# A two-layer graph network on one core: all weight loads on SyncE, and a later, wider placing of the second layer's attention chain

## The chip, the cores and the metric

The kernel runs on one NeuronCore of one Trainium2 chip. The metric is the device time of one execution in microseconds. Engines are named as in the profile: PE (TensorE), DVE (VectorE), ACT (ScalarE), POOL (GpSimd), SP (SyncE, which here only issues DMAs).

## The reference

There are 64 independent graphs of 256 nodes with 256 features, and a 256 x 256 adjacency matrix each. Two layers run one after the other on every graph, in float32.

```python
# layer 0: relational multi-head attention (8 heads of 32, 4 relations), then a feed-forward block
q, k = x @ Wq + bq, x @ Wk + bk                    # split into heads
attn = softmax(q @ k.T / sqrt(32))                 # per head
out = sum over r of (attn * (adj == r)) @ (x @ Wv[r] + bv[r])
x = LN(x + out @ Wo + bo)
x = LN(x + gelu(x @ W1 + b1) @ W2 + b2)            # 256 -> 1024 -> 256
# layer 1: two graph attentions with single scores, then a feed-forward block
def gat(h, W, a):
    Wh = h @ W
    e = leaky_relu(Wh @ a[:256] + (Wh @ a[256:]).T, 0.2)
    return softmax(where(adj > 0, e, -9e15), axis=1) @ Wh   # softmax over the row index
h = LN(x + gat(gat(x, W1', a1), W2', a2))
out = LN(h + relu(h @ w_ff1 + b1) @ w_ff2 + b2)
```

## The kernel before

Every graph is one object with a list of steps (load, x_by_feature, queries_keys, values, scores, maximum, exponential and so on). Each step issues a few instructions, mostly a PE product and the operation that takes its result out of PSUM. The method `timetable` gives every step a due time, graph g's times being shifted by g times 60. All steps of all graphs are sorted by due time (ties by order of entry) and issued in that order; every engine then runs its own instructions strictly in that order and waits by semaphores. So the due times are no clock. They only fix the order in which the steps of neighbouring graphs are interleaved: in the middle of the run, four graphs at different stages share each period.

Steps that matter here, with their lines in the kernel before:

- Weights: the helpers `weight`, `rowvec` and `colvec` (L87 to L101) and the loads in L117 to L142 each issue a DMA into a constant tile. Before, ACT issues them all, SP issues the loads of x and adj (`load_front`, L103), the residual `y` (L389) and the stores (L465).
- Layer 0: `xT` and `hT`, `ffa_T`, `ffb_T` are transposes on PE (L188) copied by ACT (L189). `qk_ps` (L302), `v_ps` (L313, evacuated by DVE in L316), scores `s` (L326), maxima `nmax` (L332, DVE), exponentials `e` (L340, ACT), reciprocals `rden` (L345, DVE), normalisation (L350, POOL), transposes of e (L356, PE), the copy `es` (L362, ACT), the masked products `pm` (L364, DVE) and the last one (L369, POOL), `po` (L380, PE; `heads_out`), `wo_ps` (L398, PE; its result is added into y by DVE, L400).
- Feed-forward blocks: ffa belongs to layer 0 (Gelu), ffb to layer 1 (Relu). `up` is L240 on PE with its activation L243 on ACT, two of eight blocks a step; `down` is L249, eight steps; `end` is L253.
- Norms (`Norm`): `stats` (L203 to L207, DVE), `root` (L211, POOL), `apply` (L216 and L220, two each, DVE). x1 and x2 follow layer 0's two halves, x3 and o layer 1's.
- Layer 1's attention chain: `gat_first` makes hT from ffa_res; `gat_product` makes `ga_wps` (L411) and its copy `ga_wh` (L413); `gat_scores` is `ga_ips` on PE (L420) and z on ACT (L423); `gat_mask` is three DVE operations (L427, L428, L430); `gat_exponential` is Exp on ACT (L435); `gat_divide` is a reciprocal and two scalings on DVE (L441, L443). `gat_second` is the product h1 on PE (L451) and its copies on ACT (L453); scores, mask, exponential and divide come again for the second attention (names gb), and `gat_out` is the product h2 (L460), added by DVE (L462).

All PE results of these steps but the scores and the accumulators of `down` share three PSUM buffers (`mm_tile`, L71), which are given out in turn.

Of the kernel before, what the change touches and what calls it, by code (L numbers as in the profile page):

```python
# [17 lines left out]
P = 128  # L18
# [5 lines left out]
def _row(ap, n):  # L24

    return bass.AP(tensor=ap.tensor, offset=ap.offset, ap=[[0, P], [1, n]])


def _col(ap, n):

    return bass.AP(tensor=ap.tensor, offset=ap.offset, ap=[[1, P], [P, n // P]])
# [3 lines left out]
def kernel(  # L35
# [12 lines left out]
    nc = tc.nc  # L48
    B, N, D = x.shape
# [4 lines left out]
    KD = D // P  # L54
# [32 lines left out]
    def weight(w, name):  # L87
        k, n = w.shape[0] // P, w.shape[1]
        t = const.tile([P, k, n], F32, name=name)
        nc.scalar.dma_start(t, w.rearrange("(k p) n -> p k n", p=P))  # L90
        return t

    def rowvec(v, n, name):
        t = const.tile([P, n], F32, name=name)
        nc.scalar.dma_start(t, _row(v, n))
        return t

    def colvec(v, n, name):
        t = const.tile([P, n // P], F32, name=name)
        nc.scalar.dma_start(t, _col(v, n))  # L100
        return t  # L101

    def load_front(g):  # L103
# [5 lines left out]

    loaded = {0: load_front(0)}  # L110
    wq, wk = weight(Wq, "wq"), weight(Wk, "wk")
    bq_c, bk_c = colvec(bq, D, "bq_c"), colvec(bk, D, "bk_c")
    scale = 1.0 / math.sqrt(DH)
    bqs_c = const.tile([P, KD], F32, name="bqs_c")
    nc.vector.tensor_scalar(bqs_c, bq_c, scale, None, op0=ALU.mult)

    wv = const.tile([P, KD, KD, R, P], F32, name="wv")  # L117
    for k in range(KD):
        for m in range(KD):
            nc.scalar.dma_start(  # L120
                wv[:, k, m], Wv[:, k * P:(k + 1) * P, m * P:(m + 1) * P].rearrange("r p n -> p r n"))
    bv_r = const.tile([P, KD, R, P], F32, name="bv_r")
    for m in range(KD):
        nc.scalar.dma_start(
            bv_r[:, m], bass.AP(tensor=bv.tensor, offset=bv.offset + m * P, ap=[[0, P], [D, R], [1, P]]))
    wo, bo_r = weight(Wo, "wo"), rowvec(bo, D, "bo_r")
    g1_r, be1_r = rowvec(g1, D, "g1_r"), rowvec(beta1, D, "be1_r")
    w1, b1_c = weight(W1, "w1"), colvec(b1, FF, "b1_c")
    w2, b2_r = weight(W2, "w2"), rowvec(b2, D, "b2_r")
    g2_r, be2_r = rowvec(g2, D, "g2_r"), rowvec(beta2, D, "be2_r")  # L130

    gw1 = bp.tile([P, KD, D], F32, tag="sT", name="gw1", bufs=3)
    nc.scalar.dma_start(gw1, gW1.rearrange("(k p) n -> p k n", p=P))
    gx = const.tile([P, KD, EX], F32, name="gx")
    nc.scalar.dma_start(gx[:, :, :D], gW2.rearrange("(k p) n -> p k n", p=P))
    a2c = const.tile([P, KD, 2], F32, name="a2c")
    for a, t, first in ((ga2, a2c, 0), (ga1, gx, D + 2)):
        for i, half in enumerate((1, 0)):
            nc.scalar.dma_start(
                t[:, :, first + i:first + i + 1],  # L140
                bass.AP(tensor=a.tensor, offset=a.offset + half * D, ap=[[1, P], [P, KD], [1, 1]]),
            )  # L142
    gext = const.tile([P, KD, EX], F32, name="gext")
    gl1_r, bl1_r = rowvec(g_ln1, D, "gl1_r"), rowvec(b_ln1, D, "bl1_r")
    f1, bf1_c = weight(w_ff1, "f1"), colvec(b_ff1, FF, "bf1_c")
    f2, bf2_r = weight(w_ff2, "f2"), rowvec(b_ff2, D, "bf2_r")
    gl2_r, bl2_r = rowvec(g_ln2, D, "gl2_r"), rowvec(b_ln2, D, "bl2_r")
# [31 lines left out]
    def at(t, f, *args):  # L179
        plan.append((t, len(plan), f, args))  # L180
# [74 lines left out]
    class Graph:  # L255
# [211 lines left out]
        def timetable(self):  # L467
            g = self.g
            t0 = g * PERIOD

            def to(t, f, *args):
                at(t0 + t, f, *args)

            def norm(t, src, gain, shift, name):
                n = Norm(gain, shift, name)
                to(t, lambda: n.stats(src()))
                to(t + 1.5, n.root)
                to(t + 3.5, n.apply)

            def ffn(t_begin, t, f, src):  # L480
                to(t_begin, lambda: f.begin(src()))
                for i in range(KF // 2):
                    to(t + 3.75 * i, f.up, 2 * i)
                for i in range(KF):
                    to(t + 15.0 + 1.875 * i, f.down, i // 4, 2 * (i % 4))
                to(t + 30.0, f.end)

            to(-20.0, self.load)
            to(14.0, self.x_by_feature)
            to(17.0, self.adj_transposed)  # L490
            to(20.0, self.queries_keys, 0)
            to(24.0, self.queries_keys, 1)
            for r in range(R + 1):
                to(29.0 + 2.0 * r, self.mask, r)
            for m in range(KD):
                s = 38.0 + 30.0 * m
                to(s, self.scores, m)
                to(s - 6.0, self.values, m, 0)
                to(s - 3.0, self.values, m, 1)
                for h in range(HQ):  # L500
                    to(s + 1.5 + 0.75 * h, self.maximum, m, h)
                    to(s + 2.5 + 1.4 * h, self.exponential, m, h)
                    to(s + 5.5 + 1.5 * h, self.reciprocal, m, h)
                    to(s + 6.0 + 1.5 * h, self.normalise, m, h)
                    to(s + 11.0 + 3.0 * h, self.transposed, m, h)
                    to(s + 11.7 + 3.0 * h, self.masked, m, h)
                    to(s + 12.5 + 3.0 * h, self.masked_last, m, h)
                to(s + 26.5, self.heads_out, m)
            to(70.0, self.load_residual)
            to(85.0, self.residual_bias)  # L510
            to(97.0, self.out_product)
            norm(98.0, lambda: self.y, g1_r, be1_r, f"x1_{g}")
            self.ffa = Ffn(w1, b1_c, AF.Gelu, w2, b2_r, f"ffa{g}")
            ffn(110.0, 113.0, self.ffa, lambda: self.y)
            norm(143.2, lambda: self.ffa.r, g2_r, be2_r, f"x2_{g}")
            to(151.0, self.gat_first)
            to(153.0, self.gat_product)
            for t, left, name in ((155.5, D + 3, f"ga{g}"), (166.5, D + 1, f"gb{g}")):
                to(t, self.gat_scores, left - 1, left, name)
                to(t + 1.3, self.gat_mask, name)  # L520
                to(t + 4.0, self.gat_exponential, name)
                to(t + 6.0, self.gat_divide, left - 1, name)
            to(164.0, self.gat_second)
            to(176.0, self.gat_out)
            norm(177.0, lambda: self.ffa.r, gl1_r, bl1_r, f"x3_{g}")
            self.ffb = Ffn(f1, bf1_c, AF.Relu, f2, bf2_r, f"ffb{g}")
            ffn(192.0, 203.0, self.ffb, lambda: self.ffa.r)
            norm(241.5, lambda: self.ffb.r, gl2_r, bl2_r, f"o{g}")
            to(248.0, self.store)

# [36 lines left out]
```

## Time and profile before

| what | value |
|---|---|
| median of 3 runs | 4270.71 us (4270.35 to 4270.79) |
| profiled execution | 4268.45 us |
| its span, first to last instruction | 4266.7 us |
| PE busy | 4007.8 us, 94% |
| DVE busy | 2848.3 us, 67% |
| ACT busy | 2001.4 us, 47% |
| POOL busy | 2024.4 us, 47% |
| mean granted TensorE clock | 0.994 |

The busy shares are means over the whole span. The page's 40 slices show PE at 5 and 8 tenths in the first two slices and at 9 or more until the last, so a short start and a long even middle have to be read apart. The DMA row shows traffic of note in the first slice only. A wait is shown in brackets behind the instruction that waited, with its length and the instruction that ended it.

### The profile page before, as it was taken

What the parts mean: (1) busy time and instruction counts of PE and PEld (TensorE: products, weight loads), DVE (VectorE), ACT (ScalarE), POOL (GpSimd) and SP (SyncE); (2) the same over time, 40 slices, a digit from 0 to 9 for tenths busy, and PEclk for the clock granted to TensorE, in tenths of its full rate; (3) what the DMA queues carried; (4) which work ended last, traced back from release to release, by engine and by line L of the source; (5) the groups of instructions that cost most, each with busy time, mean ns of one, the idle gap of its engine ahead of it and who ended that gap; (6) DMA issues with size and microseconds to landing.
All of it is one profiled execution on the core that took longest, in us unless ns stands there. A gap on an engine that the chain in (4) does not pass through costs nothing.

```text
span 4266.7 us, 67951 instructions
## 1 busy us (share of the span) xinstructions
PE 4007.8 (94%) x26136; PEld 2998.8 (70%) x26136; DVE 2848.3 (67%) x5129; ACT 2001.4 (47%) x5441; POOL 2024.4 (47%) x2374
## 2 busy tenths in 40 slices
PE   5899999999999999999999999999999999999997
PEld 3677777777777777777777777777777777777776
DVE  3576776766766767667767667667676677676674
ACT  2344544544544444445445445444444444454442
POOL 4344454455455455444444454554554454445441
PEclk9999999999999999999999999999999999999998
DMA  3000000000000000000000000000000000000000
GB/s 108 6 11 21 21 11 21 21 11 21 21 11 21 21 11 21 11 21 21 11 21 21 11 21 21 11 21 21 11 21 14 18 21 11 21 21 11 21 11 8
DMA packets 82405, 80.01 MB, mean 19 GB/s; under 512 B 8224, under 2 KB 81568, under 8 KB 82080
## 3 DMA queue, kind: packets, MB, share of 16 engines
q1 hardware_dynamic: 69632, 67.13, 5.0%
q10 hardware_dynamic: 12448, 8.54, 0.7%
q8 instruction: 206, 3.38, 0.3%
q14 instruction: 119, 0.97, 0.1%
HBM read 58.87 MB, written 16.78 MB: 18 GB/s over the span
## 4 chain that ended last, share of the span: by engine, by line
PE 64%; DVE 17%; ACT 11%; issue 4%; POOL 0%; ACTq 0%; POOLq 0%; DVEq 0%
PE v_ps L313 11%; PE po L380 11%; PE ffa_po L249 10%; PE ffa_ps L240 8%; PE ffb_ps L240 5%; PE qk_ps L302 5%; PE h_ps L451 3%; PE ga_wps L411 3%; DVE nmax L332 3%; DVE pm L364 3%; PE h_ps L460 2%; PE s L356 2%; DVE ffa_res L216 2%; PE s L326 2%; ACT es L362 2%
## 5 line engine op out<-in xcount | busy, mean ns | idle before, releaser
L364 DVE TENSOR_TENSOR pm<-rel,s 128x1536 f32<-128x1536 uint8 x512 | 893.1, 1745 | 248.0 <-ACT es L362 247.6
L350 POOL TENSOR_SCALAR e<-e,rden 128x256 f32<-128x256 f32 x1024 | 497.0, 503 | 793.9 <-DVE rden L345 793.9
L369 POOL TENSOR_TENSOR pm<-rell,es 128x512 f32<-128x512 bf16 x512 | 599.8, 1181 | 169.6 <-ACT es L362 169.6
L316 DVE TENSOR_TENSOR v<-v_ps,bv_r 128x512 f32<-128x512 f32 x256 | 176.5, 690 | 694.2 <-PE v_ps L313 694.2
L211 POOL TENSOR_TENSOR rs_x<-ve_x,nhalf 128x2 f32<-128x2 f32 x192 | 136.0, 708 | 1052.7 <-DVE ve_x L207 1036.2
L340 ACT ACTIVATE e<-s,nmax 128x256 f32<-128x256 f32 x1024 | 477.7, 484 | 271.4 <-DVE nmax L332 271.3
L249 PE MATMUL ffa_po<-w,ffa_h 128*128 128x256 f32 x2048 | 524.1, 384 | 0.0
L249 PE MATMUL ffb_po<-f,ffb_h 128*128 128x256 f32 x2048 | 509.9, 382 | 0.0
L313 PE MATMUL v_ps<-wv,xT 128*128 128x512 f32 x1024 | 496.6, 608 | 0.0
L240 PE MATMUL ffb_ps<-ffb_T,f 128*128 128x256 f32 x2048 | 486.0, 381 | 0.7 <-ACT ffb_T L189 0.7
L240 PE MATMUL ffa_ps<-ffa_T,w 128*128 128x256 f32 x2048 | 484.2, 379 | 1.0 <-ACT ffa_T L189 1.0
L380 PE MATMUL po<-pm,v 128*32 128x256 f32 x8192 | 471.0, 381 | 2.4 <-DVE pm L364 2.3
L240 PEld LDWEIGHTS ffa_ps<-ffa_T,w 128*128 128x128 f32 x2048 | 379.5, 190 | 75.0 <-issue 29.9
L249 PEld LDWEIGHTS ffa_po<-w,ffa_h 128*128 128x128 f32 x2048 | 364.4, 190 | 84.5 <-issue 51.0
L249 PEld LDWEIGHTS ffb_po<-f,ffb_h 128*128 128x128 f32 x2048 | 369.5, 190 | 60.5 <-issue 20.2
L243 ACT ACTIVATE ffa_h<-ffa_ps,b_c 128x256 f32<-128x256 f32 x512 | 214.7, 470 | 413.7 <-PE ffa_ps L240 412.9
L240 PEld LDWEIGHTS ffb_ps<-ffb_T,f 128*128 128x128 f32 x2048 | 376.4, 191 | 45.5 <-ACT ffb_T L189 1.1
L380 PEld LDWEIGHTS po<-pm,v 128*32 128x32 f32 x8192 | 253.6, 110 | 201.5 <-issue 42.5
L332 DVE TENSOR_REDUCE nmax<-s 128x2 f32<-128x512 f32 x512 | 322.9, 683 | 78.1 <-PE s L326 78.1
L243 ACT ACTIVATE ffb_h<-ffb_ps,bf_c 128x256 f32<-128x256 f32 x512 | 214.6, 470 | 272.9 <-PE ffb_ps L240 272.9
L362 ACT COPY es<-s 128x512 f32<-128x512 f32 x512 | 298.1, 583 | 77.9 <-PE s L356 51.2
L356 PE MATMUL s<-ident,e 128*128 128x128 f32 x2048 | 310.5, 275 | 9.1 <-POOL e L350 8.9
(111 smaller groups left out, 6025.9 us busy)
## 6 DMA issues: line engine op xcount, KB each, us to landing
xin<-in_x_dram SPq DMA_DIRECT2D x64, 256.0 KB, 3.1
adi<-in_adj_dram SPq DMA_DIRECT2D x64, 256.0 KB, 3.6
y<-in_x_dram SPq DMA_DIRECT2D x64, 256.0 KB, 2.8
out_dram<-ffb_res SPq DMA_DIRECT2D x64, 256.0 KB, 2.2
w<-in_L_gnn_W_dram ACTq DMA_DIRECT2D x2, 1024.0 KB, 8.0
f<-in_L_gnn_w_ff_dram ACTq DMA_DIRECT2D x2, 1024.0 KB, 9.7
wv<-in_L_gnn_Wv_dram ACTq DMA_DIRECT2D x4, 256.0 KB, 5.0
bv_r<-in_L_gnn_bv_dram ACTq DMA_DIRECT2D x2, 256.0 KB, 6.0
```

The source lines that it names most:

```text
L240: nc.tensor.matmul(p[:, f - f0, :], self.wa[:, k, f * P:(f + 1) * P], self.sT[:, k, :], start=(k == 0), stop=(k == KD - 1))
L243: nc.scalar.activation(self.h[:, f, :], p[:, f - f0, :], self.func, bias=self.ba[:, f:f + 1])
L249: nc.tensor.matmul(self.p[:, c, :], self.h[:, f, c * P:(c + 1) * P], self.wb[:, f, :], start=(f == 0), stop=(f == KF - 1))
L313: nc.tensor.matmul(p, self.xT[:, k, jc * P:(jc + 1) * P], wv[:, k, m].rearrange("p r n -> p (r n)"), start=(k == 0), stop=(k == KD - 1))
L332: nc.vector.tensor_reduce(self.nmax[h], self.s4[h].rearrange("p (c n) -> p c n", c=C), AX.X, ALU.max, negate=True)
L340: nc.scalar.activation(e[:, ic, :], self.s4[h][:, ic * N:(ic + 1) * N], AF.Exp, bias=self.nmax[h][:, ic:ic + 1], accum_out=self.den[h][:, ...
L350: nc.gpsimd.tensor_scalar(e[:, ic, :], e[:, ic, :], self.rden[h][:, ic:ic + 1], 1.0, op0=ALU.mult, op1=ALU.mult)
L356: nc.tensor.transpose(self.s4[h][:, jc * N + ic * P:jc * N + (ic + 1) * P], self.e[h][:, ic, jc * P:(jc + 1) * P], ident)
L362: nc.scalar.copy(self.es[h], self.s4[h])
L364: nc.vector.tensor_tensor(self.pm[h], self.rel.rearrange("p r c n -> p r (c n)"), bc(self.s4[h], [P, R - 1, C * N]), ALU.mult)
L369: nc.gpsimd.tensor_tensor(self.pm_l[h], self.rel_l.rearrange("p c n -> p (c n)"), self.es[h], ALU.mult)
L380: nc.tensor.matmul(po[hp, :], self.v[m][:, jc, r, hp], w, start=(r == 0 and jc == 0), stop=(r == R - 1 and jc == C - 1))
```

## The change

Two things change. The first: every weight DMA is issued by SP instead of ACT, and the loads of wv and bv are interleaved so that everything for the first half of the heads (m = 0) comes first. SP's list becomes: graph 0's x and adj, then all weights in the order in which the code uses them, then graph 1's x and adj, and so on. The second: due times of layer 1's attention chain move. The loads of `rowvec`, `colvec`, gw1, gx and a2c change in the same way as that of `weight`. From L125 on, a line of the changed kernel has a number one lower than before (L443 becomes L442).

```diff
-        nc.scalar.dma_start(t, w.rearrange("(k p) n -> p k n", p=P))
+        nc.sync.dma_start(t, w.rearrange("(k p) n -> p k n", p=P))
...
-    for k in range(KD):
-        for m in range(KD):
-            nc.scalar.dma_start(
-                wv[:, k, m], Wv[:, k * P:(k + 1) * P, m * P:(m + 1) * P].rearrange("r p n -> p r n"))
     bv_r = const.tile([P, KD, R, P], F32, name="bv_r")
     for m in range(KD):
-        nc.scalar.dma_start(
+        for k in range(KD):
+            nc.sync.dma_start(
+                wv[:, k, m], Wv[:, k * P:(k + 1) * P, m * P:(m + 1) * P].rearrange("r p n -> p r n"))
+        nc.sync.dma_start(
...
-            to(151.0, self.gat_first)
-            to(153.0, self.gat_product)
-            for t, left, name in ((155.5, D + 3, f"ga{g}"), (166.5, D + 1, f"gb{g}")):
+            to(153.0, self.gat_first)
+            to(155.0, self.gat_product)
+            for t, left, name in ((157.5, D + 3, f"ga{g}"), (171.0, D + 1, f"gb{g}")):
                 to(t, self.gat_scores, left - 1, left, name)
                 to(t + 1.3, self.gat_mask, name)
                 to(t + 4.0, self.gat_exponential, name)
                 to(t + 6.0, self.gat_divide, left - 1, name)
-            to(164.0, self.gat_second)
-            to(176.0, self.gat_out)
-            norm(177.0, lambda: self.ffa.r, gl1_r, bl1_r, f"x3_{g}")
+            to(168.5, self.gat_second)
+            to(182.5, self.gat_out)
+            norm(183.5, lambda: self.ffa.r, gl1_r, bl1_r, f"x3_{g}")
             self.ffb = Ffn(f1, bf1_c, AF.Relu, f2, bf2_r, f"ffb{g}")
-            ffn(192.0, 203.0, self.ffb, lambda: self.ffa.r)
+            ffn(196.5, 203.0, self.ffb, lambda: self.ffa.r)
```

More of the change, by code (lines that the diff above doesn't have):

```diff
@@ L94, in rowvec @@
         t = const.tile([P, n], F32, name=name)
-        nc.scalar.dma_start(t, _row(v, n))
+        nc.sync.dma_start(t, _row(v, n))
         return t
@@ L99, in colvec @@
         t = const.tile([P, n // P], F32, name=name)
-        nc.scalar.dma_start(t, _col(v, n))
+        nc.sync.dma_start(t, _col(v, n))
         return t
@@ L132 @@
     gw1 = bp.tile([P, KD, D], F32, tag="sT", name="gw1", bufs=3)
-    nc.scalar.dma_start(gw1, gW1.rearrange("(k p) n -> p k n", p=P))
+    nc.sync.dma_start(gw1, gW1.rearrange("(k p) n -> p k n", p=P))
     gx = const.tile([P, KD, EX], F32, name="gx")
-    nc.scalar.dma_start(gx[:, :, :D], gW2.rearrange("(k p) n -> p k n", p=P))
+    nc.sync.dma_start(gx[:, :, :D], gW2.rearrange("(k p) n -> p k n", p=P))
     a2c = const.tile([P, KD, 2], F32, name="a2c")
@@ L138 @@
         for i, half in enumerate((1, 0)):
-            nc.scalar.dma_start(
+            nc.sync.dma_start(
                 t[:, :, first + i:first + i + 1],
```

## The prediction, made before the changed kernel had run

> **What bounds the kernel now.** I read the windows first, then PE's waits, then one period of the timeline, then the start. The windows of 400 to 4000 us show a steady state: PE is busy 3447.76 of 3600 us at a granted clock of 1.00, DVE 2467.53, ACT 1733.00, POOL 1756.04. So TensorE bounds it, and only what leaves PE idle can be won. PE's waits in that window (line waited for, us in total, times, longest) are few:
>
> ```profile
> PE hT_ps L188 <- DVE ffa_res L220: 67.1, 56, 1.2
> PE h_ps L451 <- DVE ga_wh L443: 53.2, 56, 1.0
> PE h_ps L460 <- ACT ffa_h L243: 27.4, 55, 0.5
> ```
>
> All three are in the second layer's attention chain, once per graph. PE's timeline shows where (start, length, what; the wait in brackets):
>
> ```profile
> 2026.41 1.89 PE L240 MATMUL ffb_ps<-ffb_T,f 128*128 128x256 f32 x8
> 2029.50 0.85 PE L188 MATMUL hT_ps<-ident,ffa_res 128*128 128x128 f32 x4 [1.20 <-DVE ffa_res L220]
> ...
> 2041.11 1.89 PE L398 MATMUL wo_ps<-wo,oT 128*128 128x256 f32 x8
> ...
> 2048.68 1.98 PE L451 MATMUL h_ps<-ga_wh,ga_z 128*128 128x258 f32 x8 [0.95 <-DVE ga_wh L443]
> ...
> 2059.06 1.53 PE L460 MATMUL h_ps<-gb_wh,gb_z 128*128 128x256 f32 x6 [0.50 <-ACT ffa_h L243]
> ```
>
> The same pieces recur every 64.86 us (the m=0 heads_out product, L380, starts at 2003.00 and 2067.86). The cost of a wait is more than its bracket, since a released matmul also loses its overlap with the one before. I sum PE's start-to-start times (v_ps 1.72, ffb or ffa up 1.73, po 3.59, ga_wps 1.75, h1 1.82, h2 1.73, wo 1.73, a down pair 0.865, scores 1.08, a transpose 0.44) from the end of the third ffb up product (X = 2028.14) to the next po at 2067.86: 35.85 us of work in 39.72. So **3.9 us per period** are lost now.
>
> The start is the other idle time. ACT's timeline:
>
> ```profile
> 35.44 0.44 ACTq L95 DMA_DIRECT2D bl_r<-in_L_gnn_b_ln_dram  x1
> 35.91 1.28 ACT L189 ACT_TABLE_LOAD   x1 [35.91 <-DMA bf_c<-in_L_gnn_b_ff_dram]
> 37.21 0.59 ACT L189 COPY xT<-xT_ps 128x512 f32<-128x512 f32 x1
> ```
>
> The transposes of x were ready at 5.45 us (PE, 4.36 for 1.09), but ACT issues all weight DMAs first[...]; its first copy is at 37.21, the first scores (L326) at 47.38.
>
> [...]the next activation starts 1.30 after the load (2056.83, 2058.13). [...]the data rate (295 GB/s at 0.99 DMA share in the first 25 us) should stay. [...]a pair of L216 takes 0.88 with POOL idle (2048.71), 1.93 beside POOL (2027.03).
>
> **Part 1, weights on SP.** 34 DMA issues leave ACT and stand on SP between graph 0's and graph 1's loads. In the new order ACT can load its table and copy xT at about 5.5. Next limit: bq_c. It is now SP's fifth issue, at 0.72 + 4 x 0.5 = 2.7, and lands 5.4 later (the DMA rows), at 8.1. bqs_c and the ident_h cast stand behind it on DVE (7.21 and 7.29 now), so PE's adjacency transposes start at 8.5 instead of 7.56 and queries_keys at about 9. From queries_keys to the scores takes 47.38 - 37.85 = 9.5 now; wq, wk, the m=0 half of wv and bv_r (1.75 MB with x and adj, 6 us at 295 GB/s, and up to 6.0 from issue to landing) are there in time. Scores at 18.5: **-28.5 us**, bounds -25 (a slow bq_c) to -30.
>
> Its cost: graph 1's x now waits behind 9 MB on SP: 9.04 / 0.295 = 31 us plus landing 3.1, so 34, adj 36. PE needs it 66.96 - 47.38 = 19.6 after the first scores, at 38; 2 us of cover, a loss of at most 3 without it. y0, needed later still, is hidden too.
>
> **Part 2, the chain.** No arithmetic is added. What moves, from comparing the program orders of one period, with clock times continued from X = 2028.14 (I write 28.14):
>
> hT_ps goes behind v_ps (m=0, first half). The apply that it waits for ends at 29.75; PE has work to 29.86. Wait gone, no other: ffb up to 32.1, then po, which needs v on DVE: 31.4 + 0.65 = 32.05. ga_wps now follows po. wo ends at 41.03 against 42.84 before, of which 0.22 is ga_ips, now behind it.
>
> h1 (L451) gets worse. PE work between wo and h1: ga_ips 0.22, a down pair 0.96, scores 1.08, five pairs 4.33 = 6.6 us. On DVE the chain now runs: y add 0.72, statistics 0.67 + 0.33 + 0.09, mask 0.73 + 0.82 + 0.60, three maxima 1.80, **the four operations of norm x1's apply 1.58** (they were behind the divide, now ahead of it), fourth maximum 0.60, reciprocal 0.19, divide to PE 0.50 = 8.6, starting 0.2 after wo: 8.8. Wait 2.2 (now 0.95). ACT's exponential of ga, now behind e of head 0, ends at 47.9 against DVE's reciprocal at 49.2: hidden. h1 starts at 49.85.
>
> h2 (L460) goes from between the first two ffa up products to behind v_ps (m=1). ACT's program order holds two more table loads there per period (129 loads before, 255 after): Gelu of the first up product, load Exp (which waits for gb's maximum from DVE), gb's exponential, load Gelu. Queued behind on ACT are the es copies of heads 2 and 3 and the other Gelus, for which DVE's pm and PE's buffers wait. Chain from that product's end at 56.7: Gelu 0.9, load 1.3, two exponentials 1.0, es copy 0.56, DVE pm of head 2 1.70 (it waits for es), reciprocal and divide 0.7 = 6.2, h2 ready at 62.9. PE's cover: two transposes 0.88, two up products 3.46, v_ps 1.72 = 6.06, to 62.7. The buffer that h2 writes (three shared ones) is freed by the second Gelu at 62.6. Wait 0.2. Then the ACT delay reaches po through es, pm of head 3 and v's evacuation: DVE done 66.55, PE at 66.45: 0.1 to 0.2.
>
> New sum: 0.05 + 2.25 + 0.16 + 0.17 = 2.6 against 3.9: **-1.25 per period**. After po nothing new is late: norm x3's apply now lies between v's evacuation and the maxima, done at 74.2 when the scores end at 74.0; POOL's ffb_res (1.3) now stands inside the normalisations, whose transposes have over 5 us left. The full overlap runs from about 200 to 4130 us: 60 periods, **-75 us**. Fill and tail I take at 0, bounds -6 to +6 (the tail's own waits, such as 3.40 at h1, keep their order within one graph).
>
> Sum: -28.5 - 75 = -103.5. Against the profiled execution's 4268.45 (span 4266.7 and 1.75 around it) that is 4165; the median is 2.3 above it, so 4167.
>
> **The rivals.**
> 1. Only the start is won (about 4242): the chain's waits move and their sum stays near 3.9. For it: h1's wait doubles, and ACT and DVE covers of 0.1 to 0.3 us are thin. Against: hT's 1.36 + 0.25 is covered by a whole v_ps.
> 2. Most waits vanish (4167 - 60 x 1 = 4107): if y's add and statistics finish sooner than summed. Against: the 8.6 us are measured start-to-start times in one FIFO.
> 3. Slower: the two table loads. They add 2.6 us of ACT per period. If gb's divide meets POOL's reads, as it does now (L443 at 2056.99 took 1.92 for two), or the load of Exp waits for gb's maximum, h2 is late by 1.3 or more and pm of head 3, v's evacuation and po with it. Slower begins where the new waits reach 3.9 + 28.5/60 + 0.14 = 4.5 per period, 1.9 above my sum; at 1.0 above that, 4340. Against: POOL is idle at 62.3 in my working, and the maximum is ready at 57.3, before Gelu ends at 57.6.
> 4. The change doesn't do what it says: "order of need" may fail if one SP queue feeds the engines slower. Then graph 1's x is late: +5 at most, about 4172.
>
> **How the numbers follow.** Forecast 0.55 (rival 4 lies within it), rival 1 0.20, rival 2 0.12: together 0.87 for faster. Rival 3 0.09. The 0.04 between rivals 1 and 3, where the chain loses about what the start wins, is the chance of no change. The range leaves out these 0.13 and the outer ends of rivals 1 and 2: 4112 (2.2 us won per period) to 4242 (nothing won per period). 0.2% is 8.5 us, about what a measurement of this kernel can tell from no change: within it 0.04.
>
> **What would show it.** ACT's first copy near 5.5, scores near 18.5; a period of 63.6 instead of 64.86; no wait at hT; h1's wait over 2 us behind L442 (the divide, one line up); 255 table loads; h2 and po with short waits. Wrong: a period over 64.9, or h2 waiting over 1.5 us.

## The result and the profile after

| kernel | median us | lowest to highest | runs |
|---|---|---|---|
| before | 4270.53 | 4267.72 to 4270.79 | 4 |
| after | 4340.78 | 4340.43 to 4342.45 | 4 |

The change makes the kernel slower: ratio 1.0167, 95% interval [1.0149, 1.0184]. The forecast of 4167 was wrong in its direction.

The start went as forecast, or a little better. One line each of ACT's and PE's timelines of the kernel after (start, length, what, wait in brackets):

```profile
4.78 0.58 ACT L188 COPY xT<-xT_ps 128x512 f32<-128x512 f32 x1 [2.78 <-PE xT_ps L187]
16.90 1.15 PE L325 MATMUL s<-kT,qT 32*128 32x256 f32 x16
```

The first copy is at 4.78 instead of 37.21, the first scores at 16.90 instead of 47.38: 30.5 us earlier. Graph 0's wo product (L397) starts at 56.77 against 89.05, still 32.3 us earlier. Graph 63's starts at 4250.94 against 4178.66: 72.3 us later. So about 105 us were lost in 63 periods. The period, 64.86 us in all graphs before, is now 65.81 in one and 67.37 in another, about by turns; the mean from graph 0 to graph 63 is 4194.17 / 63 = 66.57.

The side cost of the loads was misjudged, without harm. Graph 1's x was to be there at 34 us and its adj at 36, with PE in need of them at 38. PE's timeline shows that x came late:

```profile
35.41 1.15 PE L325 MATMUL s<-kT,qT 32*128 32x256 f32 x16
39.35 1.05 PE L187 MATMUL xT_ps<-ident,xin 128*128 128x128 f32 x4 [2.79 <-DMA xin<-in_x_dram]
40.85 0.61 PE L273 MATMUL aT_ps<-ident_h,adb 128*128 128x128 bf16 x4 [0.45 <-POOL adb L266]
```

SP issued this load at 32.31, and the first 25 us moved 257 GB/s where the kernel before moved 295, a rate that, by the author's estimate, was to stay. PE waits 2.79 us for it. But the next product, aT, waits for POOL's adb in both kernels and starts 5.44 us after the scores in both (40.85 - 35.41 here, 71.32 - 65.88 before), so nothing is lost.

PE's two large waits in the kernel after, 400 to 4000 us (line waited for: us in total, times, longest):

```profile
PE h_ps L450 <- ACT e L339: 111.1, 54, 2.1
PE h_ps L459 <- DVE gb_wh L442: 98.5, 54, 2.0
```

The wait at hT is gone, as forecast, and h1 (L450) waits 2.06, near the forecast 2.2. But h2 (L459) waits 1.8 in the mean, where 0.2 was expected. PE's timeline shows two h2 in succession, and what one of them has behind it:

```profile
2014.91 2.97 PE L459 MATMUL h_ps<-gb_wh,gb_z 128*128 128x256 f32 x8 [1.94 <-DVE gb_wh L442]
2017.68 2.61 PE L239 MATMUL ffa_ps<-ffa_T,w 128*128 128x256 f32 x8
...
2056.70 1.89 PE L397 MATMUL wo_ps<-wo,oT 128*128 128x256 f32 x8
...
2067.32 1.98 PE L450 MATMUL h_ps<-ga_wh,ga_z 128*128 128x258 f32 x8 [2.06 <-ACT e L339]
...
2078.45 1.88 PE L312 MATMUL v_ps<-wv,xT 128*128 128x512 f32 x4
2082.28 1.97 PE L459 MATMUL h_ps<-gb_wh,gb_z 128*128 128x256 f32 x8 [1.95 <-DVE gb_wh L442]
2084.08 1.89 PE L239 MATMUL ffa_ps<-ffa_T,w 128*128 128x256 f32 x8
```

The h2 at 2014.91 and the product behind it take 2.97 and 2.61; the next pair of the same products takes 1.97 and 1.89. That is the difference of the two periods, and the windows name it (length, then busy us of PE, PEld, DVE, ACT, POOL with the number of instructions, then granted clock, DMA share, GB/s):

```profile
2012.30:2015.71 3.41, 1.47 (x6) 0.75 (x5) 2.98 (x5) 3.38 (x7) 1.65 (x2) 1.00 0.00 0
2015.72:2019.12 3.40, 3.40 (x10) 2.69 (x9) 3.37 (x8) 0.16 (x1) 1.36 (x2) 0.50 0.02 5
2080.56:2083.96 3.40, 1.68 (x8) 1.53 (x9) 3.22 (x5) 2.67 (x6) 1.72 (x2) 1.00 0.00 0
2083.98:2087.38 3.40, 3.35 (x38) 2.25 (x40) 3.33 (x11) 0.84 (x2) 0.70 (x1) 1.00 0.00 0
```

After the first h2 TensorE's granted clock is 0.50 for one stretch of 3.41 us; after the second it stays 1.00. The kernel after has 32 such stretches between 400 and 4000 us, the kernel before none between 180 and 4160. The mean clock hides them: the page's row of slices shows nines from end to end, and the mean of the steady windows is 0.98.

Why is h2 late? DVE's timeline ahead of it:

```profile
2066.81 0.62 DVE L442 TENSOR_SCALAR ga_wh<-ga_wh,ga_rden 128x258 f32<-128x258 f32 x2
...
2072.43 2.97 DVE L426 SCALAR_TENSOR_TENSOR gb_z<-gb_z 128x512 f32<-128x512 f32 x1 [0.23 <-ACT gb_z L422]
...
2079.91 1.75 DVE L363 TENSOR_TENSOR pm<-rel,s 128x1536 f32<-128x1536 uint8 x1 [0.70 <-ACT es L361]
2081.78 0.62 DVE L442 TENSOR_SCALAR gb_wh<-gb_wh,gb_rden 128x256 f32<-128x256 f32 x2
```

The leaky ReLU of the second attention (L426, one operation on gb_z with two SBUF inputs) takes 2.97 us. The groups of gb_z on DVE show that this is the rule (least, median and most ns), first before, then after:

```profile
L427 DVE SCALAR_TENSOR_TENSOR gb_z<-gb_z x56: 811/814/818, 431.0 to 3998.5; 128x512 f32<-128x512 f32 x56
```

```profile
L426 DVE SCALAR_TENSOR_TENSOR gb_z<-gb_z x54: 691/2970/2975, 406.6 to 3937.1; 128x512 f32<-128x512 f32 x54
```

POOL's timeline of the kernel after, at the same time:

```profile
2071.33 1.27 POOL L231 TENSOR_TENSOR ffa_res<-y,b_r 128x512 f32<-128x512 f32 x1
2072.57 2.28 POOL L368 TENSOR_TENSOR pm<-rell,es 128x512 f32<-128x512 bf16 x2
```

POOL runs ffa_res and the masked products of heads 0 and 1 without a gap, to 2074.85; L426 starts at 2072.43 and ends at 2075.40, 0.55 after POOL's last. The delay goes on through ACT (timeline, next lines):

```profile
2077.02 1.28 ACT L434 ACT_TABLE_LOAD   x1 [1.64 <-DVE gb_max L429]
2078.32 0.51 ACT L434 ACTIVATE gb_z<-gb_z,gb_max 128x256 f32<-128x256 f32 x1
2079.32 0.56 ACT L361 COPY es<-s 128x512 f32<-128x512 f32 x1
```

The Exp table load waits 1.64 for the maximum of the late mask; the copy of es queued behind it holds DVE's pm of head 2, and that stands ahead of the divide on DVE. The mask's 2.97 is a time beside POOL's tensor_tensors. Beside POOL's tensor_scalar (L350), which has its input in SBUF too, the same operation takes 0.81 in the kernel before (2052.79), little over the 0.69 that the first attention's mask takes there with POOL idle (2042.24).

### The profile page after: what moved, and what is told of

Read it like the earlier page. It is cut to its first block, busy times and chain, and to the rows that moved or that the text cites. A ratio compares the mean times of both kernels' runs of the same rounds, so it can differ in the third digit from the quotient of the medians.

```text
span 4338.9 us, 68010 instructions
## 1 busy us (share of the span) xinstructions
PE 4037.6 (93%) x26136; PEld 3046.3 (70%) x26136; DVE 2827.6 (65%) x5129; ACT 2154.0 (50%) x5567; POOL 2022.4 (47%) x2374
## 4 chain that ended last, share of the span: by engine, by line
PE 65%; DVE 17%; ACT 12%; issue 2%; POOL 0%; ACTq 0%; DVEq 0%; POOLq 0%
PE po L379 10%; PE ffa_po L248 10%; PE ffb_ps L239 10%; PE v_ps L312 8%; PE qk_ps L301 5%; ACT e L339 4%; DVE gb_z L426 4%; PE s L355 3%; PE h_ps L450 3%; PE ga_wps L410 3%; DVE pm L363 3%; PE wo_ps L397 3%; PE ffa_ps L239 2%; PE h_ps L459 2%; ACT L434 2%
## 5 line engine op out<-in xcount | busy, mean ns | idle before, releaser
L349 POOL TENSOR_SCALAR e<-e,rden 128x256 f32<-128x256 f32 x1024 | 470.8, 478 | 946.8 <-DVE rden L344 946.8
L339 ACT ACTIVATE e<-s,nmax 128x256 f32<-128x256 f32 x1024 | 473.1, 482 | 435.2 <-DVE nmax L331 435.2
L248 PE MATMUL ffa_po<-w,ffa_h 128*128 128x256 f32 x2048 | 514.0, 384 | 0.0
L239 PE MATMUL ffa_ps<-ffa_T,w 128*128 128x256 f32 x2048 | 509.1, 394 | 0.1
L210 POOL TENSOR_TENSOR rs_x<-ve_x,nhalf 128x2 f32<-128x2 f32 x192 | 168.5, 878 | 698.6 <-DVE ve_x L206 698.6
L248 PE MATMUL ffb_po<-f,ffb_h 128*128 128x256 f32 x2048 | 490.1, 383 | 0.0
L239 PEld LDWEIGHTS ffa_ps<-ffa_T,w 128*128 128x128 f32 x2048 | 397.1, 201 | 55.0 <-ACT ffa_T L188 0.5
```

Of the source, the lines that this page charges most:

```text
L239: nc.tensor.matmul(p[:, f - f0, :], self.wa[:, k, f * P:(f + 1) * P], self.sT[:, k, :], start=(k == 0), stop=(k == KD - 1))
L248: nc.tensor.matmul(self.p[:, c, :], self.h[:, f, c * P:(c + 1) * P], self.wb[:, f, :], start=(f == 0), stop=(f == KF - 1))
L339: nc.scalar.activation(e[:, ic, :], self.s4[h][:, ic * N:(ic + 1) * N], AF.Exp, bias=self.nmax[h][:, ic:ic + 1], accum_out=self.den[h][:, ...
L349: nc.gpsimd.tensor_scalar(e[:, ic, :], e[:, ic, :], self.rden[h][:, ic:ic + 1], 1.0, op0=ALU.mult, op1=ALU.mult)
```

## The experiments

The theory after this reading: (a) L426 meets POOL's products, h2 comes 2 us late; (b) PE's idle stretch of nearly 2 us brings half clock on top. Rivals: SP's order of loads slows the steady state; the two added table loads make h2 late; the waits alone, without the clock, cost all.

**One part at a time.** The first kernel has the loads of after with the due times of before, the second the reverse.

> The changed weight loads with the timetable of before. Theory (the start is won whole, and the loss is all in the timetable): the first scores near 16.9 us as in the changed kernel, a period of 64.86 us as before, so 4270.5 - 32 = about 4238 us. Rival (the weight loads on SP also cost something in the middle of the run, by graph 1's late inputs or by SP's waits): a period above 64.86 or a wait for a DMA after 40 us, and a time nearer to 4270.

> The weight loads of before with the changed timetable. Theory: the two parts add up, so 4340.8 + 32 = about 4373 us, with first scores at 47.4 and periods alternating between 65.8 and 67.4 us as in the changed kernel. Rival (the two parts interact, for instance because graph 1's inputs now arrive late): a time well below 4373.

Loads alone: 4239.08 us (4238.31 to 4240.48), ratio 0.9926 [0.9911, 0.9941]; period 64.87, waits as before. Timetable alone: 4376.35 (4373.32 to 4378.02), ratio 1.0246 [1.0231, 1.0261], with 34 half-clock stretches. The parts add up to within 4 us: -31.5 and +105.8 make +74, measured +70. The loads are worth what the start shows, and the loss is the timetable's.

**POOL's two products taken away from L426.** The products of heads 0 and 1 of m=0 become memsets (those parts of the result are left out):

```
-            nc.gpsimd.tensor_tensor(self.pm_l[h], self.rel_l..., self.es[h], ALU.mult)
+            if m == 0 and h < 2:
+                nc.gpsimd.memset(self.pm_l[h], 0.0)
+            else:
+                nc.gpsimd.tensor_tensor(self.pm_l[h], self.rel_l..., self.es[h], ALU.mult)
```

> The changed kernel, with GpSimd's masked product of the last relation replaced by a GpSimd memset for the first two heads of each graph's first half; so that relation is left out for these heads. The memset reads nothing. Theory (contention: DVE's leaky ReLU of the second attention, L426, waits for these two GpSimd products, 2.97 us instead of about 0.8, and makes h2 late): L426 falls to about 0.8, the wait at h2 from 1.94 to under 0.4, no windows at half clock remain, and the period is near 64.0 us: about 4185 us. Rival (the two added table loads on ACT set h2): L426 may fall, but the wait at h2 stays near 1.9 and the time near 4340.

Measured 4239.11 (4237.69 to 4240.49), ratio 0.9926 [0.9911, 0.9940]. Its DVE and PE timelines:

```profile
2025.82 0.74 DVE L429 SCALAR_TENSOR_TENSOR gb_z<-gb_z 128x512 f32<-128x512 f32 x1 [0.23 <-ACT gb_z L425]
```

```profile
2034.05 1.97 PE L462 MATMUL h_ps<-gb_wh,gb_z 128*128 128x256 f32 x8 [0.33 <-DVE gb_wh L445]
...
2050.53 0.40 PE L273 MATMUL aT_ps<-ident_h,adb 128*128 128x128 bf16 x4 [0.69 <-POOL adb L266]
```

The mask operation falls from 2.97 to 0.74 (L429 in this kernel), h2's wait from 1.94 to 0.33, and no half-clock stretch is left: 102 us less than after. Part (a) is shown. The forecast of 4185 was missed, and a wait of 0.69 appeared at aT. As the timelines read, ACT's Exp table load for the second half's exponentials begins only when its row maximum is there (2046.36, after 4.46 us of waiting), where in the kernel after the same load runs at 2024.34 without a wait. That this delay makes aT late was not tested, and why the load moved isn't settled.

**Are the table loads to blame?** Gelu becomes Relu in ffa (`AF.Gelu` to `AF.Relu`; the block then computes another function), so the loads between Gelu and Exp should go: of the 255 in the kernel after, 1.28 us each, none stands ahead of ffb's Relu.

> The changed kernel with Relu in place of Gelu in the first feed-forward block (Gelu is left out), so that ACT needs no change of tables in the period. Theory (contention sets h2, the table loads come second): L426 stays at 2.97, the wait at h2 falls from 1.94 by the one load on the chain, less what DVE has to do anyway, to about 1.2; 4250 to 4300 us, depending on how many windows at half clock remain. Rival (the table loads are the cause): the wait at h2 is under 0.3 and the time near 4185 us.

4239.99 (4239.40 to 4242.71), ratio 0.9929 [0.9913, 0.9946]: a little under the expected range. The timelines of DVE and PE:

```profile
2027.60 2.98 DVE L426 SCALAR_TENSOR_TENSOR gb_z<-gb_z 128x512 f32<-128x512 f32 x1 [0.24 <-ACT gb_z L422]
```

```profile
2036.66 1.97 PE L459 MATMUL h_ps<-gb_wh,gb_z 128*128 128x256 f32 x8 [1.16 <-DVE gb_wh L442]
```

The mask still takes 2.98. Without the loads h2's wait falls by 0.8, from 1.94 to 1.16; with the memsets it fell by 1.6. So the loads are a part of its chain, and the mask's delay is the larger one. No half-clock stretch follows h2's wait of 1.16; the 10 of this kernel all follow h1.

**Is the clock a cost of its own?** PE gets useless work in its idle time: one product of `values` (m=1, first half) is computed twice.

```
-            for k in range(KD):
-                nc.tensor.matmul(p, ...)
+            for _ in range(2 if (m, jc) == (1, 0) else 1):
+                for k in range(KD):
+                    nc.tensor.matmul(p, ...)
```

> The changed kernel with the value product of m = 1, first half of the nodes, computed twice in a row, so that PE has 1.72 us more work just ahead of the 1.94 us wait at h2; the result is the same. Theory (the long periods of 67.4 us come from windows at half clock that PE's idle gaps call up, and PE isn't what h2 waits for): the wait at h2 shrinks to about 0.2, every period is 65.8 us, no window of half clock remains in the middle, and the kernel with more work is faster: about 4294 us. Rival (the clock is dropped for another reason, or PE's work is on the path): 4340 or, if the product adds to the path, up to 4450 us.

4323.93 (4319.46 to 4324.54), ratio 1.0125 [1.0111, 1.0139]; 4294 was expected. With 1.72 us more work per period it is 17 us faster than after. The short periods stay at 65.80; but 22 half-clock stretches remain, now behind h1, whose wait of 2.06 was untouched, and a period with one takes 66.89. So the filler was put into both gaps: besides the above, one pair of ffb's `down` ahead of h1 is computed three times.

```
+            last = 2 if self.func == AF.Relu and (c, f0) == (1, 0) else 0
+            for i in range(last + 1):
                 for f in range(f0, f0 + 2):
                     nc.tensor.matmul(self.p[:, c, :], ...)
```

> The changed kernel with PE work added ahead of both waits: the value product of m = 1 computed twice as in e5, and ffb's first down pair of the second half of the nodes computed three times, 1.73 us more just ahead of h1; each repetition overwrites the one before, so the result is the same. Theory (a window at half clock follows when PE is idle for about 1.95 us or more within one window of 3.41 us of a fixed grid; one such window costs 1.1 to 1.6 us): with gaps of about 0.3 us at h1 and h2 no window at half clock remains in the middle, every period is 65.8 us, about 4293 us, with 3.45 us more PE work in each period than the changed kernel. Rival (the half clock has another cause[...]): the windows at half clock stay, 4320 to 4340 us or more.

4297.40 (4296.95 to 4298.74), ratio 1.0068 [1.0053, 1.0083]. PE's waits at h1 and h2, 400 to 4000 us:

```profile
PE h_ps L453 <- ACT e L342: 17.5, 54, 0.3
PE h_ps L462 <- DVE gb_wh L445: 12.7, 55, 0.2
```

Every period is 65.80 and no stretch is at half clock. **3.45 us of useless TensorE work per period made the kernel 43 us faster than after** (4340.78 - 4297.40): the engines' order is the same, only the idle time is filled. Part (b) is shown. Its size in the kernel after: the mean period of 66.57 less the undisturbed 65.80, times some 60 periods, about 46 us.

**Moving the mask.** In the kernel after, four operations of norm x1's apply stand ahead of the first attention's divide. Putting the apply behind it brings h1 and the second attention forward:

```
-            norm(98.0, lambda: self.y, g1_r, be1_r, f"x1_{g}")
+            to(98.0, lambda: n1.stats(self.y))
+            to(99.5, n1.root)
+            to(103.6, n1.apply)
```

> The changed kernel with norm x1's apply (four DVE operations) due at 103.6 instead of 101.5, that is behind ga's divide, as it stood before the change. Theory (the wait at h1 is DVE's queue, lengthened by these four operations): the wait at h1 falls from 2.06 to about 0.5. The wait at h2 is not touched by the cause, but its collision with GpSimd may shift. With the smaller gap no windows at half clock: 4200 us, up to 4290 if the half clock stays. Rival (h1 waits for ACT's exponentials, as the trace names it): the wait stays near 2.

4144.96 (4142.38 to 4145.98), ratio 0.9707 [0.9694, 0.9721], better than expected. Its PE timeline:

```profile
2040.88 1.98 PE L450 MATMUL h_ps<-ga_wh,ga_z 128*128 128x258 f32 x8 [0.84 <-DVE ga_wh L442]
...
2054.65 1.97 PE L459 MATMUL h_ps<-gb_wh,gb_z 128*128 128x256 f32 x8 [0.72 <-DVE gb_wh L442]
```

Moving one step on DVE is worth 196 us against after: h1 loses 1.2 of its wait, h2 1.2, and no half-clock stretch is left. The mask takes 1.74 here. Whether it still meets the masked products was tested by joining this edit with the memsets:

> e6 and e3 together: the changed kernel with norm x1's apply behind ga's divide, and the GpSimd product of the last relation replaced by a memset for two heads (left out there). Theory (the two causes add, and the half clock is gone already in e6): L426 falls from 1.74 to about 0.75 and the h2 wait from 0.72 to nothing, the h1 wait stays at 0.84; a wait at the adjacency transposes of up to 0.7 us may appear as in e3; period 62.6 to 63.4, 4095 to 4145 us. Rival (the table loads still hold h2): the h2 wait stays near 0.7, 4145 us.

A miss: 4185.46 (4184.83 to 4186.06), ratio 0.9806 [0.9791, 0.9820]. POOL's and DVE's timelines tell why:

```profile
2063.81 1.27 POOL L231 TENSOR_TENSOR ffa_res<-y,b_r 128x512 f32<-128x512 f32 x1
```

```profile
2063.89 1.74 DVE L429 SCALAR_TENSOR_TENSOR gb_z<-gb_z 128x512 f32<-128x512 f32 x1 [0.24 <-ACT gb_z L425]
```

In this place the mask meets ffa_res (L231), which is no memset: POOL ends at 65.08, the mask at 65.63, again 0.55 later. Taking the products away then gains nothing, and the wait of 0.69 at aT comes back.

**Less of the change.** What the waits of before ask for is small: hT 1.5 us later, and little else. The first kernel moves only hT and ga_wps in before's order, with SP's loads (`gat_first` 151 to 152.5, `gat_product` 153 to 154.4); the second also makes the first divide earlier, h2 later and norm x3 later:

```
+            to(152.5, self.gat_first)
+            to(154.4, self.gat_product)
...
+                to(t + (4.5 if left == D + 3 else 6.0), self.gat_divide, left - 1, name)
...
+            to(177.2, self.gat_out)
+            norm(178.0, lambda: self.ffa.r, gl1_r, bl1_r, f"x3_{g}")
```

> The changed weight loads with the timetable of before, and of the chain's due times only the first two moved: hT behind v_ps (152.5) and its product behind the last ffb up product (154.4). Theory (the hT wait can be had by itself): the 1.20 us wait at hT goes and the waits at h1 (0.95) and h2 (0.5) stay, a period of 63.7 us, about 4166 us. Rival (the time won comes back as a longer wait at h1, h2 or po): the period stays near 64.9, 4239 us.

> The weight loads on SP with the timetable of before and four due times moved, one for each wait: hT behind v_ps (152.5) and its product behind the last ffb up product (154.4); ga's divide between the first and the second maximum (t + 4.5); gat_out behind the second ffa up product (177.2) with norm x3 from 178. gb's mask and exponential stay where they were, ahead of the first Gelu. Theory: the hT wait (1.6 with its lost overlap), the h1 wait (1.1) and the h2 wait (1.0) go, a period of 61.5 to 62.5 us, 129 table loads as before: 4040 to 4100 us. Rival (DVE, ACT or the PSUM buffers then set other waits of the same size, as in the changed kernel): 4200 us or more.

hT only: 4151.16 (4150.51 to 4151.51), ratio 0.9725 [0.9709, 0.9742]; the hT wait is gone, 0.95 at h1 and 0.50 at h2 stay, and the period is 63.46. All three: **4064.06 (4063.61 to 4064.98), ratio 0.9519 [0.9506, 0.9532]**, faster than both kernels. PE's waits, 400 to 4000 us, are these alone:

```profile
PE hT_ps L187 <- DVE ffa_res L219: 3.2, 1, 3.2
PE gb_ips L419 <- ACT gb_wh L452: 1.4, 9, 0.2
PE h_ps L450 <- DVE ga_wh L442: 0.4, 1, 0.4
```

The period is 62.13, and PE is busy 3580.63 of 3600 us. There are 129 table loads, as before, and the mask takes 0.82.

## Why the prediction was wrong

A table of one period shows the working. "Brackets" is the sum of the brackets at h1, h2, hT and aT. The remainder is PE's own work and what waits cost beyond their brackets.

| kernel | period | brackets | added PE work | remainder |
|---|---|---|---|---|
| before | 64.86 | 2.65 | | 62.21 |
| hT only | 63.46 | 1.45 | | 62.01 |
| all three moves | 62.13 | 0 | | 62.13 |
| after, short period | 65.81 | 4.00 | | 61.81 |
| memsets | 64.85 | 3.08 | | 61.77 |
| apply late | 63.40 | 1.56 | | 61.84 |
| both fillers | 65.80 | 0.55 | 3.45 | 61.80 |

1. **The step that failed first is h2: "h2 ready at 62.9 ... Wait 0.2".** Its chain starts at the end of Gelu, because gb's maximum was put "ready at 57.3, before Gelu ends at 57.6". That holds only if the mask takes about 0.8, as in the trace of before. The order change set the mask beside POOL's ffa_res and masked products, where it takes 2.97. The prediction's clock and this trace's differ by 17.39 us (wo ends at 41.03 in the one, at 2058.42 in the other). On it the maximum came at 59.56 instead of 57.3, and h2 began at 64.89 instead of 62.9. Rival 3 named two ways for h2 to be late. One, gb's divide meeting POOL's reads, didn't come: the divide took 0.62. The other, the Exp load waiting for gb's maximum, came: it waited 1.64. The prediction had the effect from the trace, with a pair of L216 at 1.93 beside POOL and 0.88 without, but did not apply it to the mask. From start to start, v_ps at 2078.45 and h2 at 2082.28 lie 3.83 apart, where v_ps takes 1.72: 2.1 lost where the sum has 0.16, so about +2.0 per period.
2. **Half clock was not in the sum.** No step asked what a gap does to TensorE after it. It costs 1.56 in a long period and 0.8 in the mean.
3. **The rest of the sum held.** "The cost of a wait is more than its bracket" is right: hT in the kernel before lost 1.36 for a bracket of 1.20 (2026.41 to 2029.50, less the 1.73 of an up product), h2 here 2.11 for 1.95, about 0.16 more each time. That the period fell from 64.86 to 62.13 with all three moves, 2.73 for 2.65 of brackets, does not speak against it, for in that kernel PE still waits, mostly too briefly for a bracket:

```profile
1937.21 1.03 PE L248 MATMUL ffb_po<-f,ffb_h 128*128 128x256 f32 x4
1938.39 0.60 PE L419 MATMUL gb_ips<-ident,gb_wh 128*128 128x128 f32 x2
```

From start to start a down pair takes 0.865; here it is 1.18. With gb_ips 0.43 instead of 0.22, a transpose 0.82 instead of 0.44 (1939.69 to 1940.51) and the last ffb up 1.86 instead of 1.73 (1981.73 to 1983.59), 1.0 us is lost. 62.13 - 1.0 is 61.1 us of work; the prediction's sum has 64.86 - 3.9 = 61.0.

So of the 3.0 us between the forecast period of 63.6 and the measured mean of 66.6, h2 is 2.0 and the half clock 0.8. The 0.2 left is small terms, the largest of them 0.19 at aT (2031.66 to 2032.29, where four transposes take 0.44), which the sum did not have. Over 60 periods 3.0 us are 180; the time missed by 174, and the start was 2 to 4 better than forecast.

What held: the start (-28.5 forecast, -30.5 measured at the scores); no net loss from graph 1's x, though it came at 39.3 us and not at 34; the wait at hT gone; h1's wait of 2.2 (2.06 measured), set by DVE's queue as summed. The profile names ACT's e L339 as what ended it, but the divide on DVE ends at 2067.43, beside h1's start at 2067.32, and moving only DVE's apply shortens it to 0.84. The two table loads of rival 3 are a part of h2's lateness (0.8 of 1.94). That its figure of 4340 is what was measured is in part luck: it stands for new waits of 2.9 us above the sum, where h2 gave 2.0 and the half clock, which the rival does not have, 0.8. The marks set down for failure, "a period over 64.9, or h2 waiting over 1.5 us", both came.

## What to carry to other kernels

An order change moves an operation to other neighbours, so a duration from the old trace can't be taken over without a look at the new neighbours: the mask, a DVE scalar_tensor_tensor with two SBUF inputs, took 0.81 beside POOL's tensor_scalar and 2.97 beside its tensor_tensors. For such an operation in a moved chain, look what POOL runs at that time in the new order. A tensor_scalar between SBUF tiles belongs there too: gb's divide took 1.92 beside POOL's ffa_res and masked product in the kernel before, and 0.62 in the kernel after. Move only the step that waits and by as little as covers it: on the same loads, three small moves ended 206 us below the kernel before (31.5 of them from the loads), the wider spread 70 above it. Where PE's waits come near 2 us, ask also for its clock in windows of a few us, since the mean over the run hid it here (0.98), and price a gap as its bracket, what is lost besides (0.16 here), and what the half clock may add (1.56 in a long period here).

## What the runs showed of the hardware

- In the kernel after, the memset kernel, the apply-late kernel and the one that joins both, the mask of the second attention, a DVE scalar_tensor_tensor (128x512, two SBUF inputs) beside POOL tensor_tensors, ended 0.55 us after one of them ended. Such an operation takes 0.69 alone (ga_z in the kernel before, 2042.24, POOL idle); 1.74 where it begins with ffa_res; 0.74 in the memset kernel, where it begins 0.19 before ffa_res ends and no tensor_tensor follows; and 2.97 where it begins 0.17 before ffa_res ends and sits out both masked products as well. In the apply-late kernel the masked products follow ffa_res without a gap too (POOL, 2047.18), yet there it came through after ffa_res (2047.77), and they took 2.74 instead of 2.28; what decides who goes first stays open. Beside POOL tensor_scalar it takes 0.81.
- In the kernel after, half clock comes on a fixed grid of 3.413 us: the 32 stretches between 400 and 4000 us are 3.41 us long and start at the same phase of it, to 0.03 us; the first, at 483.13, and the last, at 3947.66, lie 1015 times 3.4133 us apart. Of the waits at h2 in the kernel after, the 28 with 1.93 us or more of idle inside one window are followed by a window at half clock, the 22 with 1.43 to 1.92 are not (four more wait 0.32). At h1, in three kernels (after, no Gelu, one filler), those of 2.00 or more were, those up to 1.98 not. In the timetable-only kernel one wait of 1.96 and one of 2.01 were not. So in these readings the bound lies at 1.93 to 2.01 and is not sharp.
- A wait of PE cost some 0.16 us more than its bracket, from start to start: 1.36 for 1.20 (hT, before), 2.11 for 1.95 (h2, after).
- In the kernel after it mattered where the grid falls: the waits at h1 are 2.06 us, but only four of them had 2.02 or more inside one window, and only those four were followed by half clock. So the period matters: two periods of after, 65.81 + 67.37 = 133.18, come within 0.1 us of 39 grid windows, which fits long and short periods by turns. The memset kernel's 64.85 is 19 windows: its gap of 2.06 at h1 drifts little against the grid, is cut by a border (at most 1.91 in one window), and no half-clock stretch follows it. How this falls in another run of other length was not tested.
